# The token shift of two gated units by transfers within SBUF instead of products with shift matrices

## The chip, the cores and the metric

The kernel runs on one core of one Trainium2 chip. The metric is the device time of one execution in microseconds (us): the median of three runs before the change is 3268.94 us (3267.81 to 3272.49). A core has five engines with an instruction order of their own: TensorE (PE, whose weight loads are listed apart as PEld), VectorE (DVE), ScalarE (ACT), GpSimd (POOL) and SyncE (SP). Here SP issues the transfers (DMAs), and one hardware queue carries them. An engine waits for another, or for a transfer, on semaphores, and does nothing else while it waits.

## The reference, cut to what matters

The program is a decoder of several stages on 8 batches of 512 tokens with 256 channels. The change touches two of its stages, the feed-forward units of the two layers of a local transformer. One layer is, in the reference:

```python
def shift_token(t):
    t1, t2 = jnp.split(t, 2, axis=-1)
    t2 = jnp.pad(t2, ((0, 0), (1, 0), (0, 0)))[:, :-1]
    return jnp.concatenate([t1, t2], axis=-1)
...
    x = x + o @ wo                       # end of the attention
    h = shift_token(x)
    mu = h.mean(-1, keepdims=True)
    var = h.var(-1, keepdims=True)
    h = (h - mu) / jnp.sqrt(var + 1e-05) * lg + lb
    h = h @ w1 + b1
    a, g = jnp.split(h, 2, axis=-1)
    h = a * jax.nn.gelu(g, approximate=False)
    x = x + h @ w2 + b2
```

So of every token the first 128 channels stay, and the other 128 are those of the token before it (zeros for the first token of a batch). What follows is a normalization over the 256 channels, a product up to 2 x 682 hidden channels, a gate, a product down, and a residual addition.

## The kernel before, in words

**Layout.** All activations stay in SBUF in one buffer, x: 128 partitions, and along them 32 tiles of 256 channels. Batch b has tiles 4b to 4b+3, and partition p of its tile i holds token 128 i + p. One token back is therefore one partition up; for partition 0 it is partition 127 of the tile before. The rows of a batch are `rows`, [128, 4, 256].

**The shift before** (`shifted(b)`, L2041). A 128 x 128 matrix, lf_shift, moves every row of the upper 128 channels by one partition (L2047, 512 columns, four tiles at once), a second one, lf_carry, adds partition 127 of a tile to partition 0 of the next (L2048, 384 columns). Both are products on TensorE into one PSUM bank; in 32-bit floats each is recorded as two matmuls. ACT copies the bank to lf_h (L2049). The matrices are made by GpSimd at the start of the stage (L2026).

**The rest of a batch.** VectorE takes the statistics of the two halves of each tile, x's channels and lf_h (`ln_stats`, L141, L142, L146, L147), an inverse root by three rounds of small instructions (`rsqrt`, L1458 to L1462), and eight normalizations to lf_hn (`normalize`, L155). `turned(b)` transposes lf_hn on TensorE (L2064), and VectorE copies it with scale and offset to lf_hnT (L2067). `chunk(b, f, ...)` is one of six chunks of the hidden channels: products for gate and value (L2073), a gelu on ACT (L2094), and the gated value on VectorE (L2098, lf_hid; lf_tail for the last, narrow chunk). When all six are there, four groups of products go down (L2141), each followed by the residual addition into x on VectorE (L2146); in the second layer GpSimd adds a second residual, lf_x, which SP loads (L1753).

**The loop.** Chunks of batch b stand beside `shifted(b + 1)` (at chunk 0) and `turned(b + 1)` (at chunk 3). PSUM has four kinds of banks there, sc, tr, pj and po, two of each: the shift took a tr bank, as the transposes do; chunks take pj and sc, the products down po. lf_h and lf_hn have two buffers each.

**What comes ahead of it.** The stage before is the layer's attention. It is written as a generator, and so is this stage: class `Ahead` runs the first steps of the next stage while the attention is in its last six attention chunks (`ahead.step()`). These steps are the set-up, batch 0's shift with statistics and normalization, its turning, and its six chunks. This overlapped stretch is called the tail of the attention below. In it VectorE still has the attention's work: the mask additions la_e (L1926), behind which ACT takes exponentials (L1930) and TensorE the weighted values and the sums (L1937); the copies of the sums, la_total (L1970); and reciprocals of these (x_inv). For them SP issues a chain of small transfers, sums, x_sums, invs, x_wide (L3052, L3053, L3057, L3069). GpSimd multiplies with the result (la_oT, L3070), and the product with wo (L1985) and its additions into x (L1990) end the attention.

**Order.** The instructions of each engine are put into one order when the program is built: a scheduler in the framework takes the written order and moves instructions forward where their operands, buffers and banks allow. On the chip every engine goes through its own order without skipping.

Of the kernel before, what the change touches and what calls it, by code (L numbers as in the profile page):

```python
# [26 lines left out]
F32 = mybir.dt.float32  # L27
# [5 lines left out]
ALU = mybir.AluOpType  # L33
# [4 lines left out]
P = 128  # L38
B, S, C = 8, 512, 256
NST = S // P  # L40
# [1235 lines left out]
class FastDecoder(Decoder):  # L1276
# [736 lines left out]
    def local_ffn(self, l, y, ahead):  # L2013

        nc, t = self.nc, self.t
# [3 lines left out]
        with self.tc.tile_pool(  # L2019
            name="lf", bufs=2, reuse_waits="tile", side="left" if last else "right"  # L2020
        ) as pool:

            shift = self.alloc(pool, [P, P], F32, "lf_shift", bufs=1)
            carry = self.alloc(pool, [P, P], F32, "lf_carry", bufs=1)
            for m, step, base, mul in ((shift, 1, -1, -1), (carry, -P, 1 - P, 1)):
                nc.gpsimd.affine_select(  # L2026
                    out=m, in_=self.ones, pattern=[[step, P]], compare_op=ALU.is_equal, fill=0.0,
                    base=base, channel_multiplier=mul,
                )
            gb = self.alloc(pool, [P, 4], F32, "lf_gb", bufs=1)  # L2030
            b1 = self.alloc(pool, [P, 2 * NHC - 1], F32, "lf_b1", bufs=1)
            nc.sync.dma_start(gb, t["c_ln"][l])
# [3 lines left out]
            for j in range(2):  # L2036
                tails.append(self.alloc(pool, [64, S], F32, f"lf_tail{j}", bufs=1))
                nc.gpsimd.memset(tails[j][32:64, :], 1.0)
            held = {}

            def shifted(b):  # L2041

                d = held[b] = {}
                h = self.alloc(pool, [P, NST, P], F32, "lf_h")
                ps = self.pj()
                rows = y[:, b * NST : (b + 1) * NST, :]
                nc.tensor.matmul(ps, shift, rows[:, :, P:], start=True, stop=False)  # L2047
                nc.tensor.matmul(ps[:, P:], carry, rows[:, : NST - 1, P:], start=False, stop=True)  # L2048
                nc.scalar.copy(h.rearrange("p t c -> p (t c)"), ps)  # L2049
                stats = self.ln_stats(pool, lambda i: [rows[:, i, :P], h[:, i, :]], NST, "lf_ln")  # L2050
                hn = d["hn"] = self.alloc(pool, [P, NST, C], F32, "lf_hn")
                for i in range(NST):
                    self.normalize(hn[:, i, :P], rows[:, i, :P], stats, i)
                    self.normalize(hn[:, i, P:], h[:, i, :], stats, i)
                if last:
                    d["x"] = self.residual(pool, b)
# [45 lines left out]

            yield
            shifted(0)
            yield
            turned(0)
# [4 lines left out]
            with self.banks():  # L2111
# [11 lines left out]
                for b in range(B):  # L2123
                    for f in range(NHC):
                        if b:
                            chunk(b, f, self.bank)
                        if b + 1 < B:
                            if f == 0:
                                shifted(b + 1)
                            if f == 3:  # L2130
                                turned(b + 1)
                        if b >= B - 2:
                            ahead.step(2)
                    if last and b == 1:
                        self.integer_weights(self.qpool, self.w_quantized)
                    for i in range(NST):
                        ps = self.bank("po")
                        for f in range(NHC):
                            last_f = f == NHC - 1
                            src = tails[b % 2][: TAIL + 1, :] if last_f else held[b]["hid"][:, f, :]  # L2140
                            nc.tensor.matmul(  # L2141
                                ps[:, :C], src[:, i * P : (i + 1) * P], w2[: src.shape[0], f, :],
                                start=(f == 0), stop=last_f,
                            )
                        yt = y[:, b * NST + i, :]
                        nc.vector.tensor_tensor(yt, yt, ps[:, :C], ALU.add)  # L2146
                        if last:
                            nc.gpsimd.tensor_tensor(yt, held[b]["x"][:, i, :], yt, ALU.add)
                    if last:
                        self.finished(b)  # L2150
# [1176 lines left out]
```

## Time and profile before

| | us |
|---|---|
| median of three runs | 3268.94 (3267.81 to 3272.49) |
| the profiled execution | 3272.3 |
| its span, from first to last instruction | 3270.2 |
| granted TensorE clock, mean | 0.964 |
| TensorE busy | 2955.0 (90%) |
| VectorE busy | 2123.9 (65%) |
| ACT busy | 1148.6 (35%) |
| GpSimd busy | 421.9 (13%) |
| products with lf_shift, 32 | 0.592 each in the loops |
| products with lf_carry, 32 | 0.486 each in the loops |
| ACT copies to lf_h, 16 | 0.586 each in the loops |
| eight normalizations of one batch | 2.06, start to start |
| six chunks of products up, batch 1, layer 0 | 1224.91 to 1246.28, the next shift and transposes among them |
| loop of layer 0, about | 1211 to 1487 |
| loop of layer 1, about | 1951 to 2187 |

A line of a timeline reads: start, duration, engine, source line, operation, output and inputs by the program's names, shapes, how many instructions stand in the line, and in brackets how long the engine was idle before it and what released it. "SPq" is the sequencer of SP issuing a transfer. A line with a range of starts and counts gives, for one form of instruction, the smallest, the middle and the largest duration in ns. The answers on DMA count packets of all 16 DMA engines by size; a queue's share is the time of its packets, of 16 engines' time in the window. The profile's busy time of TensorE comes from modelled ends, and consecutive products overlap a little, so starts are compared with starts.

### The profile page before, as it was taken

The numbers are of one execution on the slowest core, as the hardware profiler recorded it, in microseconds if no ns is written. First come the engines' busy times: TensorE is split into PE (matmuls) and PEld (weight loads), VectorE is DVE, ScalarE is ACT, GpSimd is POOL, SyncE is SP. The second block draws the span as 40 slices with busy tenths as digits, with TensorE's granted clock in tenths as the row PEclk, the third lists the DMA queues.
The fourth block names the chain that finished last, engine by engine and source line by source line (L and its number), as shares of the span: only waits on it lengthen the run. The fifth ranks groups of instructions, "written<-read, shape, count | busy, mean of one in ns | idle before, by whom it ended". The sixth has DMA issues, their size and how long they took to land. (4 is left out here: it accounts for less than half of the span.)

```text
span 3270.2 us, 39796 instructions
## 1 busy us (share of the span) xinstructions
PE 2955.0 (90%) x14993; PEld 1503.0 (46%) x15008; DVE 2123.9 (65%) x4590; ACT 1148.6 (35%) x1599; POOL 421.9 (13%) x388
## 2 busy tenths in 40 slices
PE   8998898878988999999989999998768999994998
PEld 5642222224544555554554555554333334332665
DVE  6458888878878854367878857548797566544110
ACT  2146566643443321124343321114262443331111
POOL 1111001010011110000011011112111232122011
PEclk9999999989999999999999999999888999997999
DMA  7011211101000010001000011000411222112431
GB/s 229 1 57 44 59 52 44 34 15 53 16 20 21 21 54 0 1 0 40 14 21 21 21 53 46 14 32 1 131 59 45 79 79 72 37 47 80 116 134 57
DMA packets 122849, 156.90 MB, mean 48 GB/s; under 512 B 47415, under 2 KB 74126, under 8 KB 121367
## 3 DMA queue, kind: packets, MB, share of 16 engines
q1 hardware_dynamic: 118550, 142.67, 14.0%
q0 software_dynamic: 4096, 11.59, 0.9%
q8 instruction: 120, 1.97, 0.2%
q14 instruction: 83, 0.67, 0.1%
HBM read 107.72 MB, written 41.22 MB: 46 GB/s over the span
## 5 line engine op out<-in xcount | busy, mean ns | idle before, releaser
L1809 PE MATMUL pj<-w,la_hT 128*128 128x512 f32 x720 | 347.4, 615 | 24.3 <-DVE la_v L1814 22.3
L1661 DVE TENSOR_TENSOR x_e<-x_e,x_share 128x1024 f32<-128x1024 f32 x256 | 307.7, 1248 | 27.9 <-ACT x_e L1660 27.1
L1660 ACT ACTIVATE x_e<-sc 128x1024 f32<-128x1024 f32 x256 | 249.8, 1026 | 147.8 <-PE sc L1649 142.9
L2770 DVE TENSOR_TENSOR ma_esum<-ma_esum,ma_e 128x1024 f32<-128x1024 f32 x96 | 125.6, 1309 | 141.8 <-ACT ma_e L2762 112.0
L2762 ACT ACTIVATE ma_e<-sc,ma_bias 128x1024 f32<-128x1024 f32 x128 | 142.6, 1115 | 200.3 <-PE sc L2757 194.5
L1809 PEld LDWEIGHTS pj<-w,la_hT 128*128 128x128 f32 x720 | 129.9, 191 | 168.0 <-issue 119.5
L3070 POOL TENSOR_TENSOR la_oT<-la_o,x_wide 128x512 f32<-128x512 f32 x64 | 96.9, 1525 | 794.7 <-DMA x_wide<-invs 636.4
L1930 ACT ACTIVATE la_e<-la_e 128x1024 f32<-128x1024 f32 (+1 forms) x128 | 121.5, 951 | 184.8 <-DVE la_e L1926 184.8
L2094 ACT ACTIVATE lf_gate<-pj,lf_b 128x512 f32<-128x512 f32 (+1 forms) x82 | 56.3, 687 | 358.2 <-PE pj L2073 358.2
L1676 PE MATMUL po<-x_e,x_v 128*32 128x512 f32 x1024 | 143.9, 636 | 32.8 <-DVE x_e L1661 30.9
L2073 PE MATMUL pj<-lf_hnT,w 128*128 128x512 f32 (+1 forms) x368 | 173.5, 598 | 0.0
L1926 DVE TENSOR_TENSOR la_e<-sc,la_mask 128x1024 f32<-128x1024 f32 (+1 forms) x128 | 138.5, 1083 | 45.9 <-PE sc L1919 45.9
L1649 PE MATMUL sc<-x_q,x_k 32*128 32x512 f32 x1024 | 161.9, 672 | 0.3 <-ACT x_e L1660 0.2
L2073 PE MATMUL sc<-lf_hnT,w 128*128 128x512 f32 x336 | 155.9, 592 | 0.0
L2141 PE MATMUL po<-w,lf_hid 128*128 128x256 f32 x640 | 153.9, 386 | 0.0
L2757 PE MATMUL sc<-ma_qT,ma_kT 64*128 64x512 f32 x512 | 145.2, 644 | 0.7 <-ACT ma_e L2762 0.7
L1985 PE MATMUL pj<-w,la_oT 128*128 128x256 f32 x512 | 124.3, 389 | 21.8 <-ACT la_qkT L1855 12.7
L2780 PE MATMUL po<-ma_e,ma_v 128*64 128x512 f32 x512 | 138.5, 619 | 0.0
L1919 PE MATMUL sc<-la_qkT 64*128 64x256 f32 (+1 forms) x1024 | 134.1, 380 | 1.7 <-DVE la_e L1926 1.7
L1937 PE MATMUL po<-la_e,la_v 128*64 128x256 f32 (+1 forms) x1024 | 130.1, 375 | 3.8 <-ACT la_o L1959 3.8
L2141 PEld LDWEIGHTS po<-w,lf_hid 128*128 128x128 f32 x640 | 117.2, 190 | 34.6 <-issue 20.4
L1816 ACT ACTIVATE la_sq<-pj 128x512 f32<-128x512 f32 x120 | 71.5, 595 | 156.0 <-PE pj L1809 155.8
(482 smaller groups left out, 5200.8 us busy)
## 6 DMA issues: line engine op xcount, KB each, us to landing
x_wide<-invs SPq DMA_DIRECT2D x192, 128.0 KB
w<-in_f_w_dram SPq DMA_DIRECT2D x16, 1024.0 KB
kv<-kv_o SPq DMA_DIRECT2D x40, 256.0 KB
slots<-x_empty SPq DMA_DIRECT2D x8, 1028.0 KB
ex_rows<-slots SPq DMA_DIRECT2D x8, 1028.0 KB
x_mask<-in_x_maskT_dram SPq DMA_DIRECT2D x8, 1024.0 KB
ma_kT<-kv SPq DMA_DIRECT2D x5, 1024.0 KB
ma_v<-kv SPq DMA_DIRECT2D x5, 1024.0 KB
```

The source lines that it names most:

```text
L1649: nc.tensor.matmul(pair[r // 2][:, r % 2, :], d["k"][rows, g, kt * P : (kt + 1) * P], d["q"][rows, e, g, :], start=True, stop=True,)
L1660: nc.scalar.activation(ex, d["e"][rest][p], AF.Exp)
L1661: nc.vector.tensor_tensor(ex, ex, d["share"][:, kt, :].unsqueeze(1).broadcast_to([P, 2, 512]), ALU.mult)
L1676: nc.tensor.matmul(d["po"][32 * r : 32 * r + 32, :], d["v"][:, kt, 8 * g + 2 * r + e, :], ex[r // 2][:, r % 2, :], start=(kt == 0), stop=( ...
L1809: nc.tensor.matmul(ps, d["hT"][:, k, i * P : (i + 1) * P], wqkv[:, k, j * S : (j + 1) * S], start=(k == 0), stop=(k == 1),)
L1919: nc.tensor.matmul(ps[:, r, jj * 256 : jj * 256 + to - j * P], d["qkT"][rows, 4 + c, j * P : (j + 1) * P], d["qkT"][rows, c, j * P : to], ...
L1926: nc.vector.tensor_tensor(ex[:, :, :n_cols], ps[:, :, :n_cols], mask[:, :n_cols].unsqueeze(1).broadcast_to([P, 2, n_cols]), ALU.add,)
L2073: nc.tensor.matmul(ps[:m, :], w1[:, k, at : at + m], held[b]["hnT"][:, k, :], start=(k == 0), stop=(k == 1))
L2141: nc.tensor.matmul(ps[:, :C], src[:, i * P : (i + 1) * P], w2[: src.shape[0], f, :], start=(f == 0), stop=last_f,)
L2757: nc.tensor.matmul(ps[:, r, :], d["k"][rows, c, kt * P : (kt + 1) * P], d["q"][rows, c, :], start=True, stop=True,)
L2762: nc.scalar.activation(ex, ps, AF.Exp, bias=bias[:, b * NST + kt : b * NST + kt + 1], scale=0.125)
L2780: nc.tensor.matmul(d["po"][64 * r : 64 * r + 64, :], d["v"][:, kt, 128 * c + 64 * r : 128 * c + 64 * r + 64], ex[:, r, :], start=(kt == 0) ...
```

## The change: what it does

The two matrices, the two products and the ACT copy are gone. Two fixed buffers, lf_h0 and lf_h1, are taken once per layer, and the first row of tile 0 is cleared once in each by GpSimd (the first token of a batch has no token before it). For each batch SP issues two transfers within SBUF, into the buffer of b modulo 2: partitions 0 to 126 of the upper channels of all four tiles to partitions 1 to 127, which are 508 pieces of 512 bytes, 260,096 bytes; and partition 127 of tiles 0 to 2 to partition 0 of tiles 1 to 3, which are 3 pieces. Per program this takes out 64 recorded matmuls and 16 ACT copies, and adds 32 transfers on SP's queue. Statistics, normalization and all that follows are as before; their lines move up by a few numbers (L2064 becomes L2059, L2073 L2068, L2098 L2093, L2146 L2141).

```diff
-            shift = self.alloc(pool, [P, P], F32, "lf_shift", bufs=1)
-            carry = self.alloc(pool, [P, P], F32, "lf_carry", bufs=1)
-            for m, step, base, mul in ((shift, 1, -1, -1), (carry, -P, 1 - P, 1)):
-                nc.gpsimd.affine_select(
-                    out=m, in_=self.ones, pattern=[[step, P]], compare_op=ALU.is_equal, fill=0.0,
-                    base=base, channel_multiplier=mul,
-                )
...
+            halves = []
+            for j in range(2):
+                halves.append(self.alloc(pool, [P, NST, P], F32, f"lf_h{j}", bufs=1))
+                nc.gpsimd.memset(halves[j][0:1, 0, :], 0.0)
             held = {}
 
             def shifted(b):
 
                 d = held[b] = {}
-                h = self.alloc(pool, [P, NST, P], F32, "lf_h")
-                ps = self.pj()
+                h = halves[b % 2]
                 rows = y[:, b * NST : (b + 1) * NST, :]
-                nc.tensor.matmul(ps, shift, rows[:, :, P:], start=True, stop=False)
-                nc.tensor.matmul(ps[:, P:], carry, rows[:, : NST - 1, P:], start=False, stop=True)
-                nc.scalar.copy(h.rearrange("p t c -> p (t c)"), ps)
+                nc.sync.dma_start(h[1:, :, :], rows[: P - 1, :, P:])
+                nc.sync.dma_start(h[0:1, 1:, :], rows[P - 1 :, : NST - 1, P:])
                 stats = self.ln_stats(pool, lambda i: [rows[:, i, :P], h[:, i, :]], NST, "lf_ln")
                 hn = d["hn"] = self.alloc(pool, [P, NST, C], F32, "lf_hn")
```

## The prediction

> **What bounds the kernel now.** I read the page's first part, then the stretches of the gated units by engine, then one batch on TensorE's timeline, then who waits for the shift.
>
> ```profile
> PE 2955.0 (90%) x14993; PEld 1503.0 (46%) x15008; DVE 2123.9 (65%) x4590; ACT 1148.6 (35%) x1599; POOL 421.9 (13%) x388
> ...
> 1211.00:1487.00 276.00, 275.90 (x896) 152.94 (x894) 130.39 (x395) 51.69 (x82) 1.60 (x6) 1.00 0.05 17
> 1951.00:2187.00 236.00, 235.35 (x758) 131.18 (x757) 152.39 (x542) 32.26 (x48) 24.28 (x31) 1.00 0.09 30
> ```
>
> Columns of the stretches: length, then busy us of PE, PEld, DVE, ACT, POOL, clock. Both loops over the batches are bound by TensorE alone; what leaves it there is time saved. The shift lies on it:
>
> ```profile
> 1228.45 1.02 PE L2047 MATMUL tr<-x,lf_shift 128*128 128x512 f32 x2
> 1229.31 0.81 PE L2048 MATMUL tr<-x,lf_carry 128*128 128x384 f32 x2
> 1229.95 1.88 PE L2073 MATMUL pj<-lf_hnT,w 128*128 128x512 f32 x4
> ```
>
> From 1228.45 to 1229.95: 1.50 us for a batch. Ahead of the loops is another stage, the attention's tail, where VectorE decides: batch 0's shift, the mask additions of the last attention chunks and the last sums all go through it in one order.
>
> ```profile
> 1152.41 0.69 DVE L1970 COPY la_total<-sum 128x512 f32<-128x512 f32 x1 [0.73 <-PE sum L1937]
> 1153.46 1.22 DVE L1926 TENSOR_TENSOR la_e<-sc,la_mask 128x1024 f32<-128x1024 f32 x1 [0.35 <-PE sc L1919]
> 1160.51 0.49 DVE L141 BATCH_NORM_STATS2 lf_ln_bn<-lf_h 128x6 f32<-128x128 f32 x2 [2.10 <-ACT lf_h L2049]
> 1177.05 0.69 DVE L1970 COPY la_total<-sum 128x512 f32<-128x512 f32 x1 [3.10 <-PE sum L1937]
> 1196.41 14.50 PE L1985 MATMUL pj<-w,la_oT 128*128 128x256 f32 x64
> ```
>
> **What is removed.** 32 products and 16 ACT copies (0.587 us each; ACT is 35% busy, their saving is nothing in itself) and four selects on POOL (0.3 us, POOL idle 8.5 us before them). TensorE saves 1.50 us for each of batches 1 to 7 in two layers: 14 x 1.50 = 21.0 us. Batch 0's slots lie in tails that VectorE will set, so they count in the tail below. Two row memsets on POOL per layer are added, in the same idle time: nothing.
>
> **What one transfer costs.** Per batch 508 pieces of 512 B (127 rows, 4 tiles) and 3 pieces. Whether 16 DMA engines share the pieces, or one takes all, decides. Two answers on DMA show how a transfer is divided:
>
> ```profile
> DMA packets 8, 0.01 MB, mean 21 GB/s; under 512 B 4, under 2 KB 4, under 8 KB 8
> ...
> DMA packets 987, 2.13 MB, mean 213 GB/s; under 512 B 47, under 2 KB 730, under 8 KB 986
> ...
> DMA packets 716, 0.36 MB, mean 299 GB/s; under 512 B 16, under 2 KB 716, under 8 KB 716
> q1 hardware_dynamic: 716, 0.36, 102.6%
> ...
> DMA packets 2309, 2.17 MB, mean 136 GB/s; under 512 B 256, under 2 KB 2304, under 8 KB 2304
> q1 hardware_dynamic: 2304, 2.10, 63.1%
> ```
>
> The first (1154.2 to 1154.6) is the 4-row transfer to sums: 4 data packets and 4 below 512 B, the latter closing notes, one per engine used. The second (1480 to 1490) has two loads of 128 rows, one of 42 and one of 1: 47 notes, that is 16 + 16 + 14 + 1. So 42 rows got 14 engines, not 16: a number that divides the rows. Of 127, a prime, only 1 does. I read this as one engine for the whole transfer.
>
> The Trainium skill's page "DMA: Bandwidth & Descriptors", section "Why a DMA increments its semaphore by 16 and not by 1", says more than these rows can: the engine count is the largest up to 16 that divides both patterns' slowest dimension, and 127 partitions go to 1. No row has a transfer of 127 rows. By the page the sum is the forecast below, by an even spread it is the first rival. The same page's section "Anatomy of one DMA" puts some 2 us of fixed cost on a transfer; the row below has less, and by 2.0 the sum would be 8 us more.
>
> A piece: the third answer (640.9 to 642.1, all engines full, loads from DRAM) gives 1.2 x 16 us / 716 = 26.8 ns for 512 B. The fourth (2294 to 2310, SBUF to SBUF, 2048 pieces of 1 KB) gives 0.631 x 16 x 16 us / 2048 = 79 ns, or 39.4 per 512 B, but those write 32 partitions at a time. I take 30, nearer the row of the same piece size: 508 x 30 ns = 15.1 us (ends 13.6 and 20.0). Ahead of it 1.1 us (la_cos issued at 639.32, first packet 640.42), behind it about 0.4: landing 16.6 us after issue. Transfers behind one another on this engine land 15.1 apart. SP's issue of 32 more DMAs (0.3 to 0.6 us each) is hidden: SP is otherwise waiting.
>
> **What moves.** The instruction order of the changed program shows that the shift no longer waits for a PSUM bank, so VectorE is given the statistics of batches 0 to 4 and the normalizations of 0 to 2 ahead of the attention's last la_total. VectorE takes its instructions in order: behind each wait for lf_h stand la_e additions, for which ACT's exponentials and then TensorE wait. With two buffers, batch b's transfer is issued only after b-2 is normalized, and SP's sums chain stands behind that wait too.
>
> Tail of layer 0. SP can issue batch 0 at 1151.6 (behind lf_b, 1151.12): landing 1168.2, where VectorE waits since 1153.1. Batch 1 lands 15.1 later, 1183.3. Then VectorE has the rest of its statistics, two la_e (1.1, 0.9) and eight normalizations (2.06), 7.7 us by the rows: 1191.0, batch 2 issued, landing 1207.6. Statistics and normalization of batch 1 with one hid, 5.6: 1213.2, batch 3 issued, landing 1229.8. Batch 2's normalization, 5.2 after 1213.2, is hidden; batch 4 follows on the engine, 1244.9. Then 1.7: la_total at 1246.6 instead of 1177.05, +69.6. Meanwhile three of batch 0's six chunks (3.43 us each on TensorE) get done, which before stood between la_total and L1985: -10.3. So +59.3.
>
> Layer 1 has lf_b at 1885.64, so batch 0 lands at 1902.7; the same 78.4 us follow: 1981.1 instead of 1917.02, +64.1, less 10.3: +53.8.
>
> Loop. Batch 5 is issued once batch 3 is normalized, 4.9 us after L1985 ends, and lands at 21.5; 5.8 us of VectorE work later the first hid frees a bank: 27.3. TensorE meanwhile has batch 0's down products (to 12.7), and five up products of 1.72 until the sc banks are full: 21.3. Stall 6.0. Batches 6 and 7: issued 3.8 us after the transposes, landing 20.4, first residual addition done at 22.2; TensorE has 5.2 us of up products and two down groups (5.9) until both po banks are full: 11.1. Stall 11.1 each. Layer 0: 28.2. In layer 1 batch 5 has 1.8 us of other VectorE work in front (7.8), and batch 6 stands 34 VectorE instructions after the issue, leaving 2.4: 7.8 + 2.4 + 11.1 = 21.3.
>
> Clock. After the idle 1.78 us at 1167.89 the granted clock was 0.50 from 1169 to 1172, and a pair of product groups took about 0.7 us longer. Eight such waits per layer: 5.6.
>
> Sum: (59.3 + 28.2 - 10.5 + 5.6) + (53.8 + 21.3 - 10.5 + 5.6) = 82.6 + 70.2 = +152.8. On the profiled execution (3272.3, span 3270.2) that is 3425.1; the median of three runs, 3268.94, lies 3.4 below it, so 3422. Sixteen transfers stand in the sum, so 1 ns per piece is 16 x 0.508 = 8.1 us: 26.8 ns gives 3396, 39.4 gives 3498.
>
> **Rivals.**
> 1. Spread over the engines: 508 pieces over 16 take 1 us, landing 2.5 to 3 after issue. VectorE's work in a tail is then, by the steps above with the stretches that lay in the waits (3.2 behind batch 0's landing, 6.5 ahead of batch 2's, 2.7 behind batch 3's), 3.2 + 7.7 + 6.5 + 5.6 + 5.2 + 2.7 + 1.7 = 32.6 us and 1.5 of wait: 1187.2, +10.1, which the chunks done earlier (-10.3) give back. The loops' 21.0 stay: 3248, faster. For it: 128-row loads do spread; the 42 rows on 14 engines do not prove what a prime gets. It decides if the landing takes less than about 5 us.
> 2. One engine, slow pieces: SBUF as source as in the fourth answer, 3498. For it: the only SBUF-to-SBUF row. Against: no fight for partitions here.
> 3. One engine, but the loops cover the waits (TensorE further ahead, VectorE's 130 of 276 us leaving room): 3422 less the stalls (49.5) and their share of the clock (4): 3368. Against: the residual additions and two po banks.
> 4. The transfers change nothing measurable: gains and waits cancel, which needs a landing near 6 us. No row gives that. That the shift isn't replaced can be excluded: the products and copies are gone from the instruction order.
>
> **How the numbers follow.** A difference below 0.2% (6.5 us) can't be told from none in this kernel. Forecast 0.60, rival 2 0.14, rival 3 0.11, rival 1 0.13, no change 0.02. Slower: 0.85; faster 0.13. The range leaves out rival 1 and thin tails: from 3350 (rival 3 at 26.8 ns) to 3510 (rival 2 with the clock's share doubled).
>
> **What would show it.** lf_h transfers landing 15 to 17 us after issue; about 511 data packets and 2 closing notes per batch; VectorE's statistics waiting some 50 us in each tail for a DMA of lf_h; TensorE idle in the tails and below 276 of 276 in the loops, with clock 0.5 to 0.9 after each gap; no L2047, L2048. It is wrong if the transfer lands in 3 us, that is if 127 rows are divided over engines in another way, or if a lone engine works much faster than the 26.8 ns it has beside 15 others.

## The result, and the profile after

The changed kernel takes 3406.93 us in the median of four runs (3401.18 to 3411.21), the kernel before 3270.72 beside it (3267.81 to 3274.29): a ratio of 1.0407, with a 95% interval of 1.0392 to 1.0422. It is slower by some 133 to 136 us. The prediction was 3422, in a range from 3350 to 3510.

The profiled execution has a span of 3409.1 us, 138.9 more than before. First the engines' busy time on the page, and the stretches of 276 and 249 us that answer to the two loops (length, then busy us of PE, PEld, DVE, ACT, POOL, clock, share of DMA, GB/s):

```profile
PE 2965.1 (87%) x14944; PEld 1506.1 (44%) x14944; DVE 2114.6 (62%) x4590; ACT 1139.6 (33%) x1583; POOL 417.8 (12%) x388
...
1283.00:1559.00 276.00, 250.87 (x794) 138.34 (x792) 107.37 (x270) 45.78 (x72) 1.60 (x6) 0.95 0.03 9
2075.00:2324.00 249.00, 229.01 (x728) 128.45 (x727) 137.14 (x430) 28.16 (x41) 24.46 (x31) 0.96 0.10 31
```

TensorE has 64 matmuls less to do (the page's weight loads fall by 64, from 15,008 to 14,944) and is still busy 10 us longer, at a lower granted clock: 0.943 on average instead of 0.964. It no longer fills the loops.

Where VectorE stands still is seen in the list of waits (total, times, longest) and in its timeline. The first line below is from the whole execution, the second from the stretch 1140 to 1500; the others are the five waits for a landing in the tail of layer 0, then the last copy of the sums and the product with wo on TensorE:

```profile
DVE lf_ln_bn L141 <- DMA lf_h<-x: 167.7, 16, 13.8
...
DVE lf_ln_bn L141 <- DMA lf_h<-x: 88.5, 8, 13.8
...
1166.17 0.29 DVE L141 BATCH_NORM_STATS2 lf_ln_bn<-lf_h 128x6 f32<-128x128 f32 x1 [13.78 <-DMA lf_h<-x]
1178.70 0.29 DVE L141 BATCH_NORM_STATS2 lf_ln_bn<-lf_h 128x6 f32<-128x128 f32 x1 [9.14 <-DMA lf_h<-x]
1202.78 0.29 DVE L141 BATCH_NORM_STATS2 lf_ln_bn<-lf_h 128x6 f32<-128x128 f32 x1 [9.94 <-DMA lf_h<-x]
1223.95 0.50 DVE L141 BATCH_NORM_STATS2 lf_ln_bn<-lf_h 128x6 f32<-128x128 f32 x2 [8.45 <-DMA lf_h<-x]
1236.48 0.29 DVE L141 BATCH_NORM_STATS2 lf_ln_bn<-lf_h 128x6 f32<-128x128 f32 x1 [9.65 <-DMA lf_h<-x]
1237.91 0.67 DVE L1970 COPY la_total<-sum 128x512 f32<-128x512 f32 x1
1248.00 14.44 PE L1985 MATMUL pj<-w,la_oT 128*128 128x256 f32 x64
```

The last la_total came at 1177.05 before; now it stands behind five landings. In the loop of layer 0, TensorE's timeline has three gaps where there were none:

```profile
1290.09 3.78 PE L2068 MATMUL sc<-lf_hnT,w 128*128 128x512 f32 x4 [6.26 <-DVE lf_hid L2093]
1318.89 3.93 PE L2136 MATMUL po<-w,lf_hid 128*128 128x256 f32 x10 [9.34 <-DVE x L2141]
1361.60 4.64 PE L2136 MATMUL po<-w,lf_hid 128*128 128x256 f32 x10 [9.44 <-DVE x L2141]
```

The first waits for a gated value, the other two for a residual addition that frees a po bank, all of which stand behind VectorE's wait for lf_h. The loop of layer 1 has two such gaps:

```profile
2108.67 3.78 PE L2068 MATMUL sc<-lf_hnT,w 128*128 128x512 f32 x4 [9.09 <-DVE lf_hid L2093]
2171.16 4.46 PE L2136 MATMUL po<-w,lf_hid 128*128 128x256 f32 x10 [10.90 <-DVE x L2141]
```

And the transfer itself, in the answer on DMA for 1189 to 1202.6, in which batch 2's pieces move:

```profile
DMA packets 524, 0.29 MB, mean 21 GB/s; under 512 B 8, under 2 KB 519, under 8 KB 523
q1 hardware_dynamic: 523, 0.27, 7.1%
```

The 511 pieces of 512 bytes take 13.2 us, at 21 GB/s, with a share of 7.1% of 16 engines: about one engine's sixteenth, which is 6.25% (the recorded times of neighbouring packets overlap a little). A piece takes 13.2 us / 511 = 25.8 ns.

In layer 1 the same pieces are slower. Two stretches of 10 us, each inside one batch's transfer with no other data on the queue, the first from layer 0 (1305 to 1315), the second from layer 1 (2156 to 2166):

```profile
DMA packets 413, 0.21 MB, mean 21 GB/s; under 512 B 2, under 2 KB 413, under 8 KB 413
...
DMA packets 375, 0.19 MB, mean 19 GB/s; under 512 B 0, under 2 KB 375, under 8 KB 375
```

411 pieces against 375. Over a whole batch, the slower first pieces included, that is 25.3 to 25.8 ns a piece in layer 0 (12.9 to 13.2 us) and 27.7 to 27.8 in layer 1 (14.1 to 14.2 us); beside loads of lf_x it is up to 30.9. Why the second layer's pieces are slower is not known.

**Where the time went.** Five marks cut both executions into stretches: the issue of lf_gb in each layer, the start of the product with wo (L1985) in the tail, and the first work of the next stage.

| stretch | before, us | after, us | difference |
|---|---|---|---|
| tail of layer 0 (1150.73 to 1196.41; 1150.02 to 1248.00) | 45.7 | 98.0 | +52.3 |
| wo and loop of layer 0 (to 1487.37; to 1559.91) | 291.0 | 311.9 | +20.9 |
| attention of layer 1 up to its tail | 397.9 | 395.9 | -2.0 |
| tail of layer 1 (1885.26 to 1936.38; 1955.83 to 2060.32) | 51.1 | 104.5 | +53.4 |
| wo and loop of layer 1 (to 2212.97; to 2349.82) | 276.6 | 289.5 | +12.9 |

They sum to +137.5; 1.4 of the span's difference lie elsewhere.

### The profile page after: what moved, and what is told of

It is laid out like the page before. It is cut to its first block, busy times and chain, and to the rows that moved or that the text cites. A ratio compares the mean times of both kernels' runs of the same rounds, so it can differ in the third digit from the quotient of the medians.

```text
span 3409.1 us, 39709 instructions
## 1 busy us (share of the span) xinstructions
PE 2965.1 (87%) x14944; PEld 1506.1 (44%) x14944; DVE 2114.6 (62%) x4590; ACT 1139.6 (33%) x1583; POOL 417.8 (12%) x388
## 5 line engine op out<-in xcount | busy, mean ns | idle before, releaser
L1661 DVE TENSOR_TENSOR x_e<-x_e,x_share 128x1024 f32<-128x1024 f32 x256 | 306.6, 1243 | 27.7 <-ACT x_e L1660 26.8
L2068 PE MATMUL pj<-lf_hnT,w 128*128 128x512 f32 (+1 forms) x368 | 187.9, 638 | 54.5 <-DVE lf_hid L2093 54.4
L2068 PE MATMUL sc<-lf_hnT,w 128*128 128x512 f32 x336 | 159.7, 604 | 15.4 <-DVE lf_hid L2093 15.4
L1676 PE MATMUL po<-x_e,x_v 128*32 128x512 f32 x1024 | 142.5, 630 | 32.7 <-DVE x_e L1661 30.9
L2136 PEld LDWEIGHTS po<-w,lf_hid 128*128 128x128 f32 x640 | 121.2, 196 | 66.2 <-DVE x L2141 30.9
L1985 PE MATMUL pj<-w,la_oT 128*128 128x256 f32 x512 | 124.2, 389 | 22.6 <-ACT la_qkT L1855 12.6
L2068 PEld LDWEIGHTS pj<-lf_hnT,w 128*128 128x128 f32 (+1 forms) x368 | 70.9, 203 | 141.0 <-issue 79.9
```

The lines of the kernel that those rows point to most:

```text
L1661: nc.vector.tensor_tensor(ex, ex, d["share"][:, kt, :].unsqueeze(1).broadcast_to([P, 2, 512]), ALU.mult)
L1676: nc.tensor.matmul(d["po"][32 * r : 32 * r + 32, :], d["v"][:, kt, 8 * g + 2 * r + e, :], ex[r // 2][:, r % 2, :], start=(kt == 0), stop=( ...
L2068: nc.tensor.matmul(ps[:m, :], w1[:, k, at : at + m], held[b]["hnT"][:, k, :], start=(k == 0), stop=(k == 1))
L2136: nc.tensor.matmul(ps[:, :C], src[:, i * P : (i + 1) * P], w2[: src.shape[0], f, :], start=(f == 0), stop=last_f,)
```

## The experiments

Theory A: one DMA engine takes all pieces of the 127-row transfer, and the time that it takes, 13 to 14 us, is exposed some sixteen times. Theory B: the new order on VectorE costs, whatever a transfer takes. Theory C: SP's stuck issues cost (the timeline of the changed kernel shows SP 11 us in the issue of the second transfer; more on that below). In all experiments the differences in us are the ratio's distance from 1, times 3268.94.

### The number of engines

The 127 rows are cut in two at 112, 122 or 124; the 3 pieces stay a transfer of their own. VectorE's order is the same in the three.

```diff
-                nc.sync.dma_start(h[1:, :, :], rows[: P - 1, :, P:])
+                nc.sync.dma_start(h[1 : 112 + 1, :, :], rows[:112, :, P:])
+                nc.sync.dma_start(h[112 + 1 :, :, :], rows[112 : P - 1, :, P:])
```

With 112 rows:

> The transfer of 127 rows is cut into one of 112 rows and one of 15; rows, bytes and the order of VectorE's work stay nearly those of the changed kernel. Theory A (one DMA engine takes all 508 pieces one after another, 25.5 ns each in the changed kernel's trace, 13 us): with 16 engines the pieces take about 1 us, the three transfers of a batch land 3 to 4 us after the first issue, the waits of VectorE for lf_h fall from 168 us to under 20, and the time is 3245 to 3262, faster than the kernel before. Theory B (VectorE's new order, which puts any transfer's latency ahead of the attention's work, costs most): the time stays above 3330. Theory C (SP, stuck for 11 us in issuing the second transfer, holds up the chain of sums): SP's three issues of about 0.75 us each remain, and the time falls as under A, but the dose of the next two runs would not follow the pieces per engine.

Measured: ratio 0.9933 (0.9908 to 0.9957), 22 us faster than the kernel before. VectorE's waits for lf_h are two, 2.3 us in all. The line of the waits, and the answer on DMA for 1189 to 1191.2, one batch:

```profile
DVE lf_ln_bn L141 <- DMA lf_h<-x: 2.3, 2, 1.2
...
DMA packets 565, 0.26 MB, mean 120 GB/s; under 512 B 54, under 2 KB 565, under 8 KB 565
```

The same bytes went at 120 GB/s. Of the 54 small packets, 34 are closing notes: 16 engines for 112 rows, 15 for 15 rows and 3 for the three pieces; the other 20 are data of a transfer beside them. Theory B falls: VectorE's order is that of the changed kernel but for some 260 of the page's 4,590 instructions, and the loss is gone. By the marks the tails are 1.4 and 0.5 us longer than before, the loops 10.6 and 12.0 shorter, where seven products' slots of 1.50 us are 10.5.

With 122 rows, and with 124:

> The transfer is cut into 122 rows and 5 rows; 122 is divided by 2 and by nothing else up to 16. Theory A: two engines, 244 pieces each, 6.2 us, landing about 7.7 us after issue; each tail some 6 us longer, two loop stalls of about 2 us per layer, 21 us of products saved: 3262 to 3282. Theory B: above 3350. If a transfer of 122 rows were spread in another way (over 16 engines), the time is that of the 112 rows, below 3262.

> The transfer is cut into 124 rows and 3 rows; the largest divisor of 124 up to 16 is 4. Theory A: four engines, 124 pieces each, 3.2 us, landing about 5 us after issue; the tails 2 to 4 us longer each, no stall in the loops: 3250 to 3266, between the 112 rows and the 122 rows. Theory B: above 3340. Spread over 16 engines: the same as the 112 rows.

Measured: 1.0076 (1.0051 to 1.0102), 25 us slower, with 122 rows; 0.9997 (0.9983 to 1.0011), no difference, with 124. With 16, 4, 2 and (uncut) 1 engines the times rise in this order, and the rate of one batch's transfer with 122 rows is twice that of one engine:

```profile
DMA packets 529, 0.27 MB, mean 37 GB/s; under 512 B 14, under 2 KB 525, under 8 KB 529
```

(1187.9 to 1195.2; without the ends 45 GB/s.) The 14 small packets are 2 notes for 122 rows, 5 for 5 rows, 3 for the three pieces and 4 of the sums. But both times, by their ratios, lie above what was expected: 3268.94 x 1.0076 = 3294 against 3262 to 3282, and 3268 against 3250 to 3266 (the second by less than its interval). The marks say where: the tails are 18.4 and 20.2 us longer with 122 rows (expected 6), 11.0 and 11.1 with 124 (expected 2 to 4). I had left out that the three transfers of a batch are issued one by one, with the sums' chain in between. With 124 rows the first batch's transfers were issued at 1160.85, 1161.73 and 1163.45, and VectorE could go on at 1167.84, 7.0 us after the first. From 122 rows to the uncut transfer the step is about as theory A has it: 6.4 us longer on the engine (6.8 to 13.2), and a tail of layer 0 that is 34 us longer (64.0 to 98.0), where five landings make 32.

### Pieces on the fullest engine, or engines at work

```diff
-                nc.sync.dma_start(h[1:, :, :], rows[: P - 1, :, P:])
+                nc.sync.dma_start(h[1:62, :, :], rows[:61, :, P:])
+                nc.sync.dma_start(h[62:, :, :], rows[61 : P - 1, :, P:])
```

> The 127 rows are cut into 61 (a prime: one engine, 244 pieces) and 66 (divided by 11: 24 pieces on each of 11 engines). The fullest engine has 244 pieces and some 25 of the other transfer, about what the cut at 122 rows gave each of two engines. Theory A (pieces on the fullest engine decide): the same time as with 122 rows or up to 15 us more, 3290 to 3315. Rival (engines at work decide, here up to 11 instead of 2): below 3275, near the cuts at 112 or 124 rows.

Measured: 1.0104 (1.0079 to 1.0128), 34 us slower. The cut at 122 had 25; their intervals overlap, so the two are not told apart. The answer on DMA for 1176.4 to 1184.1 gives 535 packets at a mean of 37 GB/s, as with 122 rows, although eleven engines moved the second part (of 19 small packets, 4 belong to the sums and 3 to the three pieces; 1 + 11 are left). The fullest engine decides. What matters is not the number 127 but how many pieces the fullest engine gets; 127 and 61, both primes, gave one engine all pieces of their transfer.

### The transfers change places

```diff
-                nc.sync.dma_start(h[1:, :, :], rows[: P - 1, :, P:])
                 nc.sync.dma_start(h[0:1, 1:, :], rows[P - 1 :, : NST - 1, P:])
+                nc.sync.dma_start(h[1:, :, :], rows[: P - 1, :, P:])
```

> The two transfers of a batch change places: the 3 pieces first, the 508 pieces behind them. Theory A: the 508 pieces take as long as before, SP is stuck at whatever it issues next instead, and the time stays within 15 us of the changed kernel, 3392 to 3422. Theory C: the 3 pieces are issued at once, SP's 11 us move behind the large transfer where the sums chain or nothing follows; if SP's stuck issues are most of the loss, the time falls by more than 40 us, below 3367.

Measured: 1.0454 (1.0427 to 1.0481), 148 us slower than before, 15 more than the changed kernel: 3417 on the base of 3268.94. Theory C's gain did not come. Why it is slower rather than equal is not settled. SP's stuck issues did not go; they moved to the sums' chain, to the next batch's small transfer, and to the tables of the next stage, as in the loop of layer 0:

```profile
1279.30 0.76 SPq L2044 DMA_DIRECT2D lf_h<-x  x1
1280.11 10.97 SPq L1772 DMA_DIRECT2D la_cos<-in_c_rope_cos_dram  x1
```

VectorE's waits for lf_h are 173.1 us in all, against 167.7 in the changed kernel. So this run shows what the 508 pieces cost, wherever they stand; it does not show that SP's queue costs nothing.

### Half of the batches

Batches 0 to 4 by products and 5 to 7 by transfers, and the other way round (GpSimd makes the two matrices again, as in the kernel before):

```diff
+                if b < 5:        # the other run: b >= 5
+                    ps = self.pj()
+                    nc.tensor.matmul(ps, shift, rows[:, :, P:], start=True, stop=False)
+                    nc.tensor.matmul(ps[:, P:], carry, rows[:, : NST - 1, P:], start=False, stop=True)
+                    nc.scalar.copy(h.rearrange("p t c -> p (t c)"), ps)
+                else:
-                nc.sync.dma_start(h[1:, :, :], rows[: P - 1, :, P:])
-                nc.sync.dma_start(h[0:1, 1:, :], rows[P - 1 :, : NST - 1, P:])
+                    nc.sync.dma_start(h[1:, :, :], rows[: P - 1, :, P:])
+                    nc.sync.dma_start(h[0:1, 1:, :], rows[P - 1 :, : NST - 1, P:])
```

> Batches 0 to 4 are shifted by products as in the kernel before, batches 5 to 7 by the transfers of the changed kernel (508 pieces on one engine). Theory A with the split of the loss into tails (five waits for a landing in each) and loops (three): the tails are back to those of the kernel before, and only the loops' stalls remain, about 25 us in layer 0 and 20 in layer 1, less 1.5 us for each of six shifts: 3293 to 3320. Rival (the loops lose only because the tails have put SP's queue and TensorE's clock out of step): within 8 us of the kernel before.

> The other half: batches 0 to 4 by the transfers, 5 to 7 by products. Theory A: both tails longer by 50 to 54 us as in the changed kernel, no stall in the loops, four products' slots saved per layer (12 us): 3350 to 3375. With the run before it the differences from the kernel before should add to that of the changed kernel, 136 us, within 12 us. Rival (tails and loops lose together): the sum is off by more than 25 us.

Measured: 1.0084 (1.0063 to 1.0105), 27 us slower, for the late batches; 1.0258 (1.0235 to 1.0281), 84 us, for the early ones. Each is on the side that theory A has, with the tails as before in the one (46.0 and 50.9 us) and as in the changed kernel in the other (97.0 and 103.8). The rival, that the loops lose only in the tails' wake, falls: the late batches lose by themselves. The two add to 112, not to 133 or 136; the sum missed the 12 us that I allowed, and did not reach the 25 of the rival, that tails and loops lose together. It is the loop of layer 0 that does not add: +12.4 and -6.0 by the marks, together 6.4, against +20.9. The loop of layer 1 does: +20.0 and -7.5, together 12.5, against +12.9. In the run with the late batches VectorE waits there only twice:

```profile
1327.14 0.50 DVE L141 BATCH_NORM_STATS2 lf_ln_bn<-lf_h 128x6 f32<-128x128 f32 x2 [8.28 <-DMA lf_h<-x]
1339.67 0.29 DVE L141 BATCH_NORM_STATS2 lf_ln_bn<-lf_h 128x6 f32<-128x128 f32 x1 [8.94 <-DMA lf_h<-x]
```

Batch 5's transfer, issued at 1278.12, was there before VectorE asked for it: where a product shifts batch 4, the order leaves more work between.

### Four buffers

```diff
-            for j in range(2):
+            for j in range(4):
                 halves.append(self.alloc(pool, [P, NST, P], F32, f"lf_h{j}", bufs=1))
...
-                h = halves[b % 2]
+                h = halves[b % 4]
```

> Four buffers for the shifted halves instead of two, all else as in the changed kernel, so that a transfer need not wait until the batch two before it is normalized. Theory A: the engine still takes 13 us for each batch, and VectorE's order now has six landings ahead of the last sums, but they follow each other without the 6 to 8 us of VectorE's work between, and two of three loop stalls go: 3325 to 3370. Rival (the wait for a free buffer is most of the loss): below 3300. Rival (buffers do not matter, the engine's 13 us times 16 are all): above 3390.

Measured: 1.0414 (1.0381 to 1.0447), the same as with two, 3404 on the base. My expectation under theory A was wrong. The number lies in the range of the last rival, but buffers did matter: they moved the wait to another place. In layer 0, 1140 to 1560, VectorE waits 36 us less for lf_h than in the changed kernel, and more for the sums:

```profile
DVE lf_ln_bn L141 <- DMA lf_h<-x: 52.5, 5, 13.0
DVE x_inv L3051 <- DMA x_sums<-sums: 30.2, 2, 19.8
```

The changed kernel has 1.5 us in this second line. Over the whole execution VectorE waits 50 us less for lf_h (117.7 against 167.7 us) and 56 us more for the sums; the two lines are of the changed kernel and of this run:

```profile
DVE x_inv L3051 <- DMA x_sums<-sums: 43.0, 30, 3.3
...
DVE x_inv L3051 <- DMA x_sums<-sums: 99.0, 31, 24.9
```

SP's timeline shows what the sums stood behind (start, duration of the issue):

```profile
1166.54 11.70 SPq L3047 DMA_DIRECT2D sums<-la_total  x1
1178.29 0.72 SPq L2044 DMA_DIRECT2D lf_h<-x  x1
1179.05 0.71 SPq L2043 DMA_DIRECT2D lf_h<-x  x1
1179.82 11.04 SPq L2044 DMA_DIRECT2D lf_h<-x  x1
1190.96 0.35 SPq L3048 DMA_DIRECT2D x_sums<-sums  x1
```

The issue behind an uncut transfer lasts until most of that transfer has moved, so x_sums was issued 24.4 us after sums. In the tail of layer 0 of the changed kernel the three distances are 15.1, 14.3 and 1.7 us; in the kernel before they are 1.7, 1.7 and 2.4. With four buffers theory C's mechanism takes the place of the wait for a buffer: SP's queue is stuck with transfers that nobody needs yet, ahead of the ones that the attention needs. That this alone makes up for the gain is read from these waits; no run frees SP with four buffers and uncut transfers, so it is not shown.

### GpSimd's queue

```diff
-                nc.sync.dma_start(h[1:, :, :], rows[: P - 1, :, P:])
+                nc.gpsimd.dma_start(h[1:, :, :], rows[: P - 1, :, P:])
```

> The same 127-row transfer, uncut, but issued by GpSimd on its own queue; the 3 pieces stay with SP. It asks whether the one engine comes from the 127 rows alone or from SP's queue. If the rows alone decide: 508 pieces in a row at 25.5 ns, landing 15 us after issue, and the time stays near the changed kernel, 3370 to 3430 (a little less where SP is no longer stuck in its next issue). If GpSimd's queue divides 127 rows over all engines: some 32 pieces each, 0.8 us, landing 3 to 5 us after issue with the longer issue on GpSimd, and the time is 3250 to 3290, near the cuts at 112 and 124 rows. The Trainium skill's page "DMA: Bandwidth & Descriptors", section "Why a DMA increments its semaphore by 16 and not by 1", names GpSimd's queue on this chip as such an exception; the numbers above do not need it.

Measured: 1.0600 (1.0577 to 1.0624), 196 us slower, outside both expectations. The answer on DMA for 1198 to 1224 has:

```profile
q0 software_dynamic: 1040, 0.29, 7.5%
...
lf_h<-x POOLq DMA_DIRECT2D x1, 254.0 KB, 22.8
```

The transfer was issued in 4.6 us and landed 22.8 us after issue. Its 1040 packets are 945 of 32 bytes in the first 8 us or so of its work, 64 of 2 or 4 KB (the 260,096 bytes), and 31 smaller ones, 16 of which have the 4 bytes of a closing note. The skill's section named in the expectation has some direct copies on this queue spread over 16 engines. This one was not: from 1214.1 to 1220.6, when the 32-byte packets were through, the answer on DMA has

```profile
DMA packets 34, 0.13 MB, mean 20 GB/s; under 512 B 1, under 2 KB 1, under 8 KB 34
...
q0 software_dynamic: 34, 0.13, 6.3%
```

The data packets follow one another, a new one every 198 ns, and fill one sixteenth of 16 engines: one engine moves them, at 20 GB/s as on SP's queue. The closing notes agree: 15 of the 16 came between 1210.0 and 1211.5, in the middle of the data, and only the last one, the single small packet in the view above, behind the last data packet, at 1220.6. So sixteen notes do not mean sixteen engines with data here, and the one engine does not come from SP's queue: on both queues one engine moves the 127 rows. The landing is 7.6 us later than on SP's queue (22.8 against 15.2) for two reasons: the first data packet comes 5.5 us after the start of the issue instead of 1.4, and the data take 16.7 us instead of 13.2, since in the first half, beside the 32-byte packets, they follow each other in 160 to 930 ns. That this puts the time outside both expectations is argued, not shown. What the 32-byte packets are is not known.

### Whole rows

All 256 channels of a row, which lie 4 KB in one run for the four tiles; the lower half is copied and not read.

```diff
-                halves.append(self.alloc(pool, [P, NST, P], F32, f"lf_h{j}", bufs=1))
+                halves.append(self.alloc(pool, [P, NST, C], F32, f"lf_h{j}", bufs=1))
...
-                nc.sync.dma_start(h[1:, :, :], rows[: P - 1, :, P:])
-                nc.sync.dma_start(h[0:1, 1:, :], rows[P - 1 :, : NST - 1, P:])
+                nc.sync.dma_start(h[1:, :, :], rows[: P - 1, :, :])
+                nc.sync.dma_start(h[0:1, 1:, :], rows[P - 1 :, : NST - 1, :])
```

(The statistics and the normalization read `h[:, i, P:]`.)

> The transfer takes all 256 channels of the 127 rows (twice the bytes; the lower half is copied and not used), which in each row are 4 KB in one run: 127 pieces on the one engine, if a run becomes one piece. If the engine's time goes by pieces (25.5 ns each, or 84 as 2 KB ones took in the kernel before), the transfer takes 3 to 11 us and the time falls to 3275 to 3385. If it goes by bytes (512 bytes in 25.5 ns, 20 bytes per ns; the 6 KB loads' 26 bytes per ns as the other end), 520 KB take 20 to 26 us, 7 to 13 us more for each of 16 transfers: 3490 to 3620.

Measured: 1.0750 (1.0727 to 1.0773), 245 us slower. 1200.3 to 1221.6, one batch:

```profile
DMA packets 169, 0.55 MB, mean 26 GB/s; under 512 B 37, under 2 KB 37, under 8 KB 168
```

The 127 pieces of 4 KB take 20.9 us in this batch, 166 ns each, those of 512 bytes 25.8 ns. Eight times the bytes take 6.4 times as long, so the engine's time goes mostly by bytes: two equations give an estimate of 20 ns for 512 bytes and 6 ns for a piece. The transfer takes 7 to 8 us longer than the uncut half rows (20.9 against 13.2 us in layer 0, 21.0 to 21.2 against 14.1 in layer 1), and the kernel 112 us longer than the changed one: sixteen times 7.

## Why the prediction was right

**One engine for 127 rows: right.** The completions of the 42-row load were the hint, the rate of 21 GB/s and the cuts at 112, 122, 124 and 61 rows are the proof. The rule that the prediction cites from the Trainium skill's page "DMA: Bandwidth & Descriptors", section "Why a DMA increments its semaphore by 16 and not by 1" (the largest number up to 16 that divides the rows), agrees with the closing notes of the uncut transfer and of all four cuts on SP's queue. Only their number a batch was forecast wrongly, 2 for 4. The answer on DMA for 1211.5 to 1224, one batch of the changed kernel:

```profile
DMA packets 511, 0.26 MB, mean 21 GB/s; under 512 B 4, under 2 KB 511, under 8 KB 511
```

One note is that of the 127 rows, and three are those of the 3 pieces, which got three engines, as in all the cuts.

**A piece at 30 ns: too high, and the fixed part too low.** A piece took 25.8 ns in layer 0, below even the nearer end of 26.8 (all engines full, from DRAM), and 27.7 or more in layer 1. The time of a transfer outside its pieces was 1.9 to 2.1 us instead of the 1.1 + 0.4 of the sum: the first piece came 1.4 us after issue, and VectorE went on some 0.5 to 0.7 us behind the last. (The 2.0 us that the prediction names from the skill's section "Anatomy of one DMA" are stated there for transfers that GpSimd issues; the rows here show about as much for SP's.) So landings came 15.0 to 16.5 us after issue in layer 0 and 16.1 to 18.4 in layer 1 where VectorE waited, against 16.6 forecast. An estimate from these numbers: the pieces alone make the sum too high by 8 x 0.508 x 4.2 = 17 us in layer 0 and 8 x 0.508 x 2.2 = 9 in layer 1, the fixed part makes it too low by 16 x 0.5 = 8. Together that is 18, and the forecast was 15 over the measured median. That the two errors have opposite signs is luck.

**The tails: right in their steps.** In layer 0 +52.3 for +59.3: five landings that were each 1.4 to 2.6 us earlier than forecast. VectorE's five waits there are 51.0 us in all, where some 50 were forecast. In layer 1 +53.4 for +53.8, and there each step holds within 1.4 us. From the issue of lf_gb to the first landing it is 17.5 us for 17.4, to the last la_total 94.2 for 95.8. Batch 1's transfer was issued late (1970.49, 13.73 us after batch 0's at 1956.76), because SP was stuck for 11.75 us and then had lf_x and the sums to issue, but the engine still had pieces of batch 0 to move then, and batch 1 landed 15.6 us behind batch 0 (1973.29 and 1988.85), for 15.1.

**The loops: nearly right.** Forecast stalls were 6.0, 11.1 and 11.1 in layer 0; measured 6.26, 9.34 and 9.44. With the products' 10.5 saved and the clock, +20.9 for 23.3. In layer 1 they were 7.8, 2.4 and 11.1; measured 9.09, none and 10.90, and +12.9 for 16.4. The half-batch runs confirm the split between tails and loops in sign and in the main size, with the exception of batch 5 told above.

**The clock: right in kind.** After the first wait in layer 0 the granted clock was 0.50 (1166 to 1171), and it was 0.50 to 0.72 after four others. Its share of the loss was not measured apart.

**SP's issues: sized wrongly, and hidden for another reason.** The prediction gave the added issues 0.3 to 0.6 us each and hid them, since SP is otherwise waiting. The first transfer of a batch takes SP about 0.75 us, the second 11.6 in the middle, because it is stuck behind the 508 pieces:

```profile
1150.94 0.84 SPq L2043 DMA_DIRECT2D lf_h<-x  x1
1151.82 10.97 SPq L2044 DMA_DIRECT2D lf_h<-x  x1
1162.83 0.74 SPq L2043 DMA_DIRECT2D lf_h<-x  x1
1163.67 11.70 SPq L3047 DMA_DIRECT2D sums<-la_total  x1
```

In the changed kernel this hides behind VectorE's waits for the same transfers (1.5 us are spent waiting for the sums in layer 0); with four buffers it does not. That the forecast did not suffer from this term is luck.

**The rivals.** The spread transfer was forecast at 3248: the cut at 112 rows has 3268.94 x 0.9933 = 3247. So the price of that case was right, and its condition was what failed. Slow pieces (39.4 ns) and loops that hide the waits did not occur.

## What to carry to other kernels

Before a transfer takes the place of work on an engine, look at how many rows its outermost dimension has and count the closing notes of the nearest transfers of the same queue in the trace (on GpSimd's queue they misled): 127 rows ran on one DMA engine and cost 133 us here, the same rows cut at 112 run on sixteen and save 22. A transfer that sits on one engine also holds the issuing engine's next transfer, so whatever else that queue carries (here the sums of the attention) is late as well. And where a scheduler orders the instructions, an operand that no longer waits for a bank lets its users move ahead of other work: see what then waits behind them.

## What the runs showed of the hardware

- SP's issue of the transfer that follows one of 508 pieces on one engine lasted 10.93 to 13.44 us in the changed kernel; behind 244 pieces an engine 4.4 to 5.4, behind 124 pieces 0.9 to 2.8, behind 28 pieces 0.6 to 1.0. In 12 of the 16 batches it came free when 396 to 401 of the 508 pieces had begun to move, so with some 110 left (in the other four the pieces of the batch before are in the count). For the first batch, 1152 to 1162.79, with 18 small packets and 398 pieces:

```profile
DMA packets 416, 0.20 MB, mean 19 GB/s; under 512 B 18, under 2 KB 416, under 8 KB 416
```

- One DMA engine moved 512-byte pieces within SBUF at 20 bytes per ns in layer 0 and 18.5 in layer 1, and 4 KB pieces at 25.
- On GpSimd's queue the same transfer had 945 packets of 32 bytes at its start, data packets of 4 KB on one engine, 15 of 16 closing notes in the middle of the data, and a landing 22.8 us after issue, later than on SP's.
